# Decay from re-read rows of G, and k k^T with k q^T in one product, in an adaLN block with a gated delta rule

## The chip, the cores and the metric

The kernel runs on one core of one Trainium2 chip. The metric is the device time of one execution in microseconds (us), from start to end of the program; a profiled execution also has a span, from its first to its last instruction.

## What is computed

The block takes x of shape (8, 512, 256), 8 batch rows of 512 tokens, and computes two residual branches. The second is a small mixture of experts and is not touched. The first is gated attention with a delta rule, 16 key heads and 32 value heads of width 128:

```python
q = l2norm(q) * dk ** -0.5;  k = l2norm(k)         # each key head serves two value heads
G = cumsum(g) within a chunk
decay = where(tril, exp(G[..., :, None] - G[..., None, :]), 0.0)
A = -where(strict_tril, einsum(k_beta, k) * decay, 0.0)
T = solve_triangular(eye - A, eye, lower=True)
...
attn = where(tril, einsum(q_i, k_i) * decay, 0.0)
v_new = v_i - kcd_i @ state                        # v_i, kcd_i come from T
out_i = (q_i * exp(g_i)) @ state + attn @ v_new
```

q, k and v come from a projection of the normalised, modulated x, a causal convolution over four tokens, and SiLU; the output is normalised, gated with SiLU(z) and projected back. The kernel works with chunks of 128 tokens in place of the 64 of the reference (the result is the same), so each batch row has four chunks.

## The kernel before

Everything is fp32. The work is cut into 128 items: item n is key head `p = n % 16` of batch row `b = n // 16`, with its two value heads (h = 0, 1) and four chunks (c). One step n of the main loop (L1032 to L1069) runs five stages side by side, each for another item:

- `keys(n + 9)` (L481), the early stage: projection, convolution and SiLU of k (`projected`, L438), its transposes (`k_rows`), norms and scalars; the decays of the eight (chunk, head) pairs (`decay`, L521); k k^T (`products`, L539); their product on GpSimd (`decayed`, L551); and `leave` (L556), which writes the blocks to DRAM.
- one quarter of `diagonal_blocks` (L588) for a group of four items: the inverses of the 32x32 diagonal blocks, on VectorE, with one block in each partition. It reads the group back from DRAM in `begin` (L614); `join16_w` and `join16_x` (L664, L674) join 16-row pieces by a product and a reduction over 1024 or 2048 columns.
- `join(n + 1)` (L697): joining to 64 and 128 rows on TensorE.
- `queries(n + 1)` (L781), the late stage: projection of q and of two v, the squares and norms of q, k q^T (`products`, L819), its product with the causal mask `tri_le` (`qkm`) and with the decays (`s`, L835), and the transposes of v.
- `recur(n)` (L862), the recurrence over four chunks, and `finish(n - 1)` (L967): z, gating, the output projection (L1010).

`weave` (L38) merges the lists of steps by their relative position, so that the stages alternate in program order. Side steps (`beside`, L1025) carry the norms of the next batch row, before it is needed, and the experts of the last. The framework's planner then fixes one order for each engine's queue, from readiness of data, free buffers and program order; at run time each queue is in order. All loads and stores of the main loop go through SP's queue.

What the early stage makes for the late one goes through DRAM (pool `far`): `kfar` holds k and its transpose, `dfar` the decays, 512 KB an item. `load` of `queries` reads them back one step ahead of use.

The decay of two chunks is a TensorE product. GpSimd builds `gm` (L524), the mask times g, for 4 x 128 columns; a matmul with the mask `tri_gt` as stationary operand sums the g between two tokens (`ds`, L530); ScalarE takes Exp from PSUM (L532):

```python
nc.gpsimd.tensor_tensor(gm..., tri_le..., bc_last(rw["g"][:, 2 * gr : 2 * gr + 2, hs], P), ALU.mult)
mm(ps, tri_gt, gm.rearrange("p u i -> p (u i)"), start=True, stop=True)
nc.scalar.activation(dc.rearrange("p u i -> p (u i)"), ps, AF.Exp)
```

[...] The weights of k, of q and v (`key_weights`, `query_weights`, L423, L426) have two buffers each, z and output weights (`gate_weights`, L430) one. `out_weights` (L994) scales the output weights into a second tile `wg`.

Of the kernel before, what the change touches and what calls it, by code (L numbers as in the profile page):

```python
# [15 lines left out]
P = 128  # L16
# [32 lines left out]
def adaln_block(  # L49
# [62 lines left out]
    row = ctx.enter_context(tc.tile_pool(name="row", bufs=2))  # L112
    rows = {}
# [71 lines left out]
    def before_attention(b):  # L185
# [4 lines left out]
        def betas():  # L190
# [9 lines left out]
            d["g"] = row.tile([P, NC, HV], F32, name=f"g_{b}", tag="g")  # L200
# [27 lines left out]
        def decays():  # L228

            n = NC * HV  # L230
            ps = bank(ps_m, f"dec_{b}")
            gf = d["g"].rearrange("p c h -> p (c h)")
            for i, m in enumerate((tri_le, tri_gt, ones)):
                mm(ps[:, i * n : (i + 1) * n], m, gf, start=True, stop=True)
            ex = d["ex"] = row.tile([P, 3, NC, HV], F32, name=f"ex_{b}", tag="ex")
            nc.scalar.activation(ex.rearrange("p i c h -> p (i c h)"), ps[:, : 3 * n], AF.Exp)
            d["neg"] = row.tile([P, NC, HV], F32, name=f"neg_{b}", tag="neg")
            nc.vector.tensor_scalar_mul(d["neg"], ex[:, 0], -1.0)

        return [*norm_transposed(b, 0, 2, "a"), betas, soft, series, decays]  # L240
# [147 lines left out]
    with ExitStack() as st:  # L388
# [34 lines left out]
        def key_weights(n):  # L423
            weights(n, "wk", wp, ((HK + n % HK) * P, 1))

        def query_weights(n):  # L426
            p = n % HK
            weights(n, "wq", wp, (p * P, 1), ((2 * HK + 2 * p) * P, 2))
# [9 lines left out]
        def projected(n, parts):  # L438
# [5 lines left out]
            def one(wname, j, name, ch):  # L444
# [18 lines left out]
                def act():  # L463
                    pool = w2b if name == "q" else w1b
                    tag = "ka" if name == "k" else name
                    r = d[name] = pool.tile([P, SEQ], F32, name=f"{name}_{n}", tag=tag)
                    nc.scalar.activation(r, d["cv" + name], AF.Silu)  # L467
# [10 lines left out]
        def chunks_of(t):  # L478
            return bass.AP(t.tensor, t.offset, [[2 * NC * P, P], [1, 2 * NC * P]])

        def keys(n):  # L481
# [5 lines left out]
            def k_rows():  # L487
                ps = d["kt"] = bank(ps_m, f"kt_{n}")
                for c in range(NC):
                    nc.tensor.transpose(  # L490
                        ps[:, c * P : (c + 1) * P], d["k"][:, c * P : (c + 1) * P], ident
                    )
                kr = w1b.tile([P, NC, P], F32, name=f"kra_{n}", tag="kra")
                nc.scalar.copy(kr.rearrange("p c d -> p (c d)"), ps)
                d["kfar"] = far.tile([2, P, SEQ], F32, name=f"kfar_{n}", tag="kfar")
                nc.sync.dma_start(d["kfar"][0], d["k"])
                nc.sync.dma_start(d["kfar"][1], kr.rearrange("p c d -> p (c d)"))

            def norms():
                ps = d["kt"]  # L500
                nrm = d["nrmk"] = keep.tile([P, NC], F32, name=f"nrmk_{n}", tag="nrmk")
                for c in range(NC):
                    junk = w2b.tile([P, P], F32, name=f"jk_{n}_{c}", tag="jk")
                    nc.scalar.activation(
                        junk, ps[:, c * P : (c + 1) * P], AF.Square, accum_out=nrm[:, c : c + 1]
# [4 lines left out]
            def scalars():  # L510
# [10 lines left out]
            def decay(gr):  # L521

                gm = w1b.tile([P, 4, P], F32, name=f"gm_{n}_{gr}", tag="gm")
                nc.gpsimd.tensor_tensor(  # L524
                    gm.rearrange("p (c h) i -> p c h i", h=2),
                    tri_le.unsqueeze(1).unsqueeze(1).to_broadcast([P, 2, 2, P]),
                    bc_last(rw["g"][:, 2 * gr : 2 * gr + 2, hs], P), ALU.mult,
                )
                ps = bank(ps_m, f"ds_{n}_{gr}")
                mm(ps, tri_gt, gm.rearrange("p u i -> p (u i)"), start=True, stop=True)  # L530
                dc = d[f"dca{gr}"] = w2b.tile([P, 4, P], F32, name=f"dca_{n}_{gr}", tag="dca")
                nc.scalar.activation(dc.rearrange("p u i -> p (u i)"), ps, AF.Exp)  # L532
                if gr == 0:
                    d["dfar"] = far.tile([P, 2 * NC * P], F32, name=f"dfar_{n}", tag="dfar")
                nc.sync.dma_start(
                    d["dfar"][:, gr * SEQ : (gr + 1) * SEQ], dc.rearrange("p u i -> p (u i)")
                )

            def products():  # L539
                ps = bank(ps_m, f"kk_{n}")  # L540
                for c in range(NC):
                    cs = slice(c * P, (c + 1) * P)
                    mm(ps[:, cs], d["k"][:, cs], d["k"][:, cs], start=True, stop=True)
                v = ps.rearrange("p (c d) -> p c d", d=P)
                mt = d["mta"] = w1b.tile([P, 2 * NC, P], F32, name=f"mta_{n}", tag="mta")
                nc.vector.tensor_mul(  # L546
                    mt.rearrange("p (c h) i -> p c h i", h=2),
                    v.unsqueeze(2).to_broadcast([P, NC, 2, P]), bc_last(d["nb"], P),
                )

            def decayed(gr):  # L551
                us = slice(4 * gr, 4 * gr + 4)
                mt = d["mta"][:, us, :]
                nc.gpsimd.tensor_tensor(mt, mt, d[f"dca{gr}"], ALU.mult)  # L554

            def leave():  # L556
# [20 lines left out]
                nc.sync.dma_start(d["m6far"], mt[0:64, :, 64:128])  # L577

            return [
                *projected(n, [("wk", 0, "k", HK + p)]), k_rows, lambda: decay(0), norms, scalars,  # L580
                lambda: decay(1), products, lambda: decayed(0), lambda: decayed(1), leave,
# [6 lines left out]
        def diagonal_blocks(g):  # L588
# [25 lines left out]
            def begin():  # L614
# [4 lines left out]
                e["pr"] = w1b.tile([P, 2048], F32, name=f"prl_{g}", tag="prl")  # L619
# [32 lines left out]
            def join8_x(q):  # L652
                o = 16 * q
                wt = e["wt"][:, 64 * q : 64 * q + 64].rearrange("p (c b) -> p c b", c=8)
                pr = e["pr"][:, 1024 + 512 * q : 1536 + 512 * q].rearrange(
# [8 lines left out]
            def join16_w(k):  # L664

                pr = e["pr"][:, : 2048 >> k].rearrange("p (c a b) -> p c a b", c=8, a=16)
                mul(
                    pr, bc(minus_m(16, 8 * k, 16, 16 - 8 * k), 1, 8),
                    bc(part(yl, 8 * k, 8 * k, 8, 16 - 8 * k), 2, 16), ALU.mult,
                )  # L670
                wt = e["wt"].rearrange("p (c a) -> p c a", c=16)
                red(wt[:, 8 * k : 8 * k + 8, :], pr, AX.X, ALU.add)

            def join16_x(k):  # L674
                w = 8 + 8 * k
                pr = e["pr"][:, : 128 * w].rearrange("p (a c b) -> p a c b", a=8, c=16)
                wt = e["wt"].rearrange("p (c b) -> p c b", c=16)
                mul(
                    pr, bc(part(xl, 16 + 8 * k, 16, 8, w), 2, 16), bc(wt[:, :, :w], 1, 8), ALU.mult
                )  # L680
                red(part(xl, 16 + 8 * k, 0, 8, 16), pr, AX.X, ALU.add)

            def leave():
# [9 lines left out]
                [lambda: join16_w(0), lambda: join16_w(1)],  # L693
                [lambda: join16_x(0), lambda: join16_x(1), leave],
# [86 lines left out]
        def queries(n):  # L781

            b, p = divmod(n, HK)
            d, rw = its[n], rows[b]
            hs = slice(2 * p, 2 * p + 2)

            def load():
                d["k"] = w2b.tile([P, SEQ], F32, name=f"k_{n}", tag="k")
                nc.sync.dma_start(d["k"], d["kfar"][0])
                d["dc"] = w1b.tile([P, 2 * NC, P], F32, name=f"dc_{n}", tag="dc")  # L790
                nc.sync.dma_start(d["dc"].rearrange("p u i -> p (u i)"), d["dfar"])
                d["kr"] = w2b.tile([P, NC, P], F32, name=f"kr_{n}", tag="kr")
                nc.sync.dma_start(d["kr"].rearrange("p c d -> p (c d)"), d["kfar"][1])

            def squares():
                d["sq"] = w1b.tile([P, SEQ], F32, name=f"sq_{n}", tag="sq")
# [317 lines left out]
```

## Time and profile before

| | |
|---|---|
| median of 3 runs | 5013.29 us (5008.72 to 5019.26) |
| the profiled execution | 5009.07 us |
| its span | 5007.4 us |
| mean granted TensorE clock | 0.978 |
| GpSimd busy | 2128.2 us (43%) |
| DMA, SP's queue | 568.86 MB, 40.5% of 16 engines' span |

In a page of the profile PE is TensorE's matmuls, PEld its weight loads, DVE VectorE, ACT ScalarE, POOL GpSimd and SP the queue that issues DMAs. A row names line, engine, operation, result and sources, shapes and count; then the busy time in us and the mean ns of one; then the engine's idle time just before these instructions, and what ended it. Each fp32 matmul of the program shows as two records. `prq`, `prk` and `prv` are the banks of the projections of q, k and v, `op` that of the output.

### The profile page before, as it was taken

Reading aid. Unit: us, or ns where it says so; the run is one execution under the profiler, and the core shown is the slowest. Engines: PE = TensorE matmul, PEld = TensorE weight load, DVE = VectorE, ACT = ScalarE, POOL = GpSimd, SP = SyncE. Lnnn points to the kernel's source line nnn. Section 1 sums busy time; section 2 is a strip of 40 time slices with the busy share of each in tenths; the row PEclk is TensorE's granted clock in tenths of the full one; section 3 lists DMA queues with packets and bytes.
Section 4 is the critical chain, followed back from the end, with each engine's and each line's share of the span. In section 5 each row is a group of like instructions: output and inputs, shape, how many; then the busy total and the mean of one; then the engine's idle time right before and its main releaser. Section 6 shows DMA issues by size and latency. Waiting matters only on the chain. (4 is left out here: it accounts for less than half of the span.)

```text
span 5007.4 us, 86632 instructions
## 1 busy us (share of the span) xinstructions
PE 4749.6 (95%) x28800; PEld 3397.5 (68%) x28800; DVE 3799.0 (76%) x8080; ACT 3112.8 (62%) x8127; POOL 2128.2 (43%) x1962
## 2 busy tenths in 40 slices
PE   4799999999999999999999999999999999999998
PEld 2467776666776667766677666766766666776775
DVE  4777778877788777887777777877788776788754
ACT  3566666666666665666666676566666667656553
POOL 3344444444444434444444443444444444444432
PEclk8799999999999999999999999999999999999999
DMA  4344444444444444444344444444444444444331
GB/s 132 107 111 119 128 123 116 121 112 119 121 114 126 117 112 120 120 117 121 108 120 118 123 119 118 110 119 127 113 118 117 114 126 119 113 117 126 98 87 35
DMA packets 972522, 576.23 MB, mean 115 GB/s; under 512 B 656544, under 2 KB 836656, under 8 KB 972080
## 3 DMA queue, kind: packets, MB, share of 16 engines
q1 hardware_dynamic: 971264, 568.86, 40.5%
q8 instruction: 234, 3.83, 0.3%
q14 instruction: 208, 1.70, 0.1%
q10 hardware_dynamic: 816, 1.84, 0.1%
HBM read 356.53 MB, written 213.91 MB: 114 GB/s over the span
## 5 line engine op out<-in xcount | busy, mean ns | idle before, releaser
L952 ACT ACTIVATE jo<-o 128x128 f32<-128x128 f32 x1024 | 305.4, 299 | 679.9 <-DVE o L946 669.8
L458 DVE SCALAR_TENSOR_TENSOR cvv<-prv,cw,cvv 128x511 f32<-128x511 f32 (+2 forms) x768 | 556.7, 741 | 22.9 <-ACT cvv L456 20.3
L1010 PE MATMUL op<-wg,gt 128*128 128x256 f32 x2048 | 513.7, 390 | 10.9 <-DVE o L946 9.5
L524 POOL TENSOR_TENSOR gm<-tri_le,g 128x512 f32<-128x512 f32 x256 | 279.0, 1090 | 515.2 <-PE ds L530 505.1
L448 PE MATMUL prv<-ha,wq 128*128 128x512 f32 x1024 | 485.3, 596 | 3.0 <-DVE cvk L458 3.0
L977 PE MATMUL prz<-ha,wz 128*128 128x512 f32 x1024 | 485.6, 593 | 0.0
L797 POOL TENSOR_TENSOR sq<-q 128x512 f32<-128x512 f32 x128 | 133.0, 1039 | 793.9 <-ACT q L467 793.9
L554 POOL TENSOR_TENSOR mta<-mta,dca 128x512 f32<-128x512 f32 x256 | 325.3, 1287 | 341.6 <-DVE mta L546 199.9
L1010 PEld LDWEIGHTS op<-wg,gt 128*128 128x128 f32 x2048 | 373.2, 192 | 84.6 <-DVE o L946 14.6
L912 ACT ACTIVATE w<-u,br 128x128 f32<-128x128 f32 x1024 | 317.5, 363 | 147.4 <-PE u L897 121.1
L458 DVE SCALAR_TENSOR_TENSOR cvk<-prk,cw,cvk 128x511 f32<-128x511 f32 (+2 forms) x384 | 284.8, 742 | 159.5 <-ACT cvk L456 159.1
L835 POOL TENSOR_TENSOR s<-qkm,dc 128x256 f32<-128x256 f32 x512 | 373.5, 762 | 22.7 <-DVE qkm L826 18.2
L938 PEld LDWEIGHTS in<-w,s 128*128 128x128 f32 x2048 | 307.1, 192 | 109.0 <-issue 81.8
L467 ACT ACT_TABLE_LOAD x255 | 327.2, 1283 | 65.9 <-DVE cvk L458 42.0
L1015 DVE TENSOR_TENSOR xt<-xt,op 128x512 f32<-128x512 f32 x256 | 175.5, 685 | 250.3 <-PE op L1010 248.8
L532 ACT ACT_TABLE_LOAD x248 | 318.2, 1283 | 44.1 <-issue 36.2
L996 POOL TENSOR_TENSOR wg<-wo,ga 128x512 f32<-128x512 f32 x128 | 177.6, 1388 | 378.4 <-PE op L1010 377.3
L448 PEld LDWEIGHTS prv<-ha,wq 128*128 128x128 f32 x1024 | 192.5, 190 | 193.9 <-issue 180.9
L938 PE MATMUL in<-w,s 128*128 128x128 f32 x2048 | 319.1, 277 | 4.5 <-ACT xw L768 2.4
L530 PE MATMUL ds<-gm,tri_gt 128*128 128x512 f32 x512 | 281.0, 632 | 29.2 <-POOL gm L524 16.3
L992 POOL TENSOR_TENSOR o<-o,msq 128x512 f32<-128x512 f32 x256 | 304.4, 1210 | 10.0
L897 PEld LDWEIGHTS u<-r,y 128*128 128x128 f32 x1536 | 235.6, 194 | 94.4 <-issue 55.2
(214 smaller groups left out, 11861.9 us busy)
## 6 DMA issues: line engine op xcount, KB each, us to landing
dfar<-dca SPq DMA_DIRECT2D x256, 256.0 KB
dc<-dfar SPq DMA_DIRECT2D x128, 512.0 KB
wq<-in_dram SPq DMA_DIRECT2D x128, 256.0 KB
wz<-in_dram SPq DMA_DIRECT2D x128, 256.0 KB
wo<-in_dram SPq DMA_DIRECT2D x128, 256.0 KB
kfar<-k SPq DMA_DIRECT2D x128, 256.0 KB
kfar<-kra SPq DMA_DIRECT2D x128, 256.0 KB
k<-kfar SPq DMA_DIRECT2D x128, 256.0 KB
```

The costliest lines, as they stand in the source:

```text
L448: mm(ps, d[wname][:, kt, j * P : (j + 1) * P], hT[:, kt, :], start=kt == 0, stop=kt == NKT - 1,)
L458: nc.vector.scalar_tensor_tensor(a[:, s:], ps[:, : SEQ - s], cw[:, ch, 3 - s : 4 - s], a[:, s:], ALU.mult, ALU.add,)
L467: nc.scalar.activation(r, d["cv" + name], AF.Silu)
L532: nc.scalar.activation(dc.rearrange("p u i -> p (u i)"), ps, AF.Exp)
L554: nc.gpsimd.tensor_tensor(mt, mt, d[f"dca{gr}"], ALU.mult)
L835: nc.gpsimd.tensor_tensor(d["s"][:, u : u + 2, :], bc_mid(d["qkm"][:, c, :], 2), d["dc"][:, u : u + 2, :], ALU.mult,)
L912: nc.scalar.activation(w[:, h, :], ps[:, h * P : (h + 1) * P], AF.Copy, scale=d["br2"][:, c, h : h + 1],)
L938: mm(ps[:, h * P : (h + 1) * P], d["s"][:, 2 * c + h, :], cur["w"][:, h, :], start=True, stop=True,)
L952: nc.scalar.activation(junk, d["o"][:, c, h, :], AF.Square, accum_out=d["msq"][:, c, h : h + 1])
L977: mm(ps, d["wz"][:, kt, h * P : (h + 1) * P], hT[:, kt, :], start=kt == 0, stop=kt == NKT - 1,)
L992: nc.gpsimd.tensor_tensor(o, o, bc_last(m, P), ALU.mult)
L1010: mm(ps[:, k * DM : (k + 1) * DM], gt[h][:, c * P : (c + 1) * P], d["wg"][:, h, :], start=h == 0, stop=h == 1,)
```

## The change

The decays no longer come from a matmul. `decays` keeps G, the running sum of g within a chunk (`d["G"]`, tokens on partitions), transposes it on TensorE and writes the 128x128 result (a row for each chunk and head) to DRAM (`gfar`). For each item, `key_weights` reads the eight rows back, each copied to all 128 partitions (`gb`, one buffer). `decay` subtracts the token's own G by `tensor_scalar` on GpSimd, one instruction for each chunk and head, takes the minimum with 0, and ScalarE takes Exp in place, for both pairs of chunks in succession.

q moves from the late stage to the early one: projection, convolution, SiLU, squares, norms, scalars. k and q lie side by side in one tile `kqa` (one buffer), so one matmul with 256 columns gives k k^T and k q^T of a chunk. `products` and `decayed` work on two chunks at a time; `decayed` also makes s, which goes to DRAM (`sfar`) instead of the decays, as k and q do (`qfar`). The late stage, now `values`, has only v, and loads k with q, k's transpose, and s. To make room, `pr` of the diagonal blocks shrinks from 2048 to 1024 columns, `join16_w` and `join16_x` are cut in three pieces each, g has one buffer, and the output weights are scaled in place. `soft` and `series` become one side step.

```diff
@@ decays
+            d["G"] = row.tile([P, NC, HV], F32, name=f"G_{b}", tag="G")
+            nc.vector.tensor_copy(d["G"].rearrange("p c h -> p (c h)"), ps[:, :n])
+            ps = bank(ps_m, f"Gt_{b}")
+            nc.tensor.transpose(ps[:, :P], d["G"].rearrange("p c h -> p (c h)"), ident)
+            gt = row.tile([P, P], F32, name=f"Gt_{b}", tag="Gt", bufs=1)
+            nc.vector.tensor_copy(gt, ps[:, :P])
+            d["gfar"] = gfar.tile([P, P], F32, name=f"gfar_{b}", tag="gfar")
+            nc.sync.dma_start(d["gfar"], gt)
-        return [*norm_transposed(b, 0, 2, "a"), betas, soft, series, decays]
+        return [*norm_transposed(b, 0, 2, "a"), betas, lambda: (soft(), series()), decays]
@@ key_weights
-            weights(n, "wk", wp, ((HK + n % HK) * P, 1))
+            b, p = divmod(n, HK)
+            weights(n, "wk", wp, ((HK + p) * P, 1), (p * P, 1))
+            t = its[n]["gb"] = w1b.tile([P, NC, 2 * P], F32, name=f"gb_{n}", tag="gb")
+            far_g = rows[b]["gfar"]
+            nc.sync.dma_start(
+                t,
+                bass.AP(
+                    far_g.tensor, far_g.offset + 2 * p * P,
+                    [[0, P], [HV * P, NC], [1, 2 * P]],
+                ),
+            )
@@ keys
+            def squares():
+                d["sq"] = w1b.tile([P, NC, P], F32, name=f"sq_{n}", tag="sq")
+                nc.gpsimd.tensor_tensor(d["sq"], d["kqa"][:, :, 1, :], d["kqa"][:, :, 1, :], ALU.mult)
+                d["qfar"] = far.tile([P, 2 * SEQ], F32, name=f"qfar_{n}", tag="qfar")
+                nc.sync.dma_start(d["qfar"], d["kqa"].rearrange("p c k i -> p (c k i)"))
...
+            def decay():
+                for gr in range(2):
+                    dc = d[f"dca{gr}"] = w2b.tile([P, 2, 2, P], F32, name=f"dca_{n}_{gr}", tag="dca")
+                    for c in range(2):
+                        for h in range(2):
+                            k = 2 * p + h
+                            nc.gpsimd.tensor_scalar(
+                                dc[:, c, h, :], d["gb"][:, 2 * gr + c, h * P : (h + 1) * P],
+                                rw["G"][:, 2 * gr + c, k : k + 1], 0.0, ALU.subtract, ALU.min,
+                            )
+                for gr in range(2):
+                    f = d[f"dca{gr}"].rearrange("p c h i -> p (c h i)")
+                    nc.scalar.activation(f, f, AF.Exp)
+
+            def products(gr):
+                ps = bank(ps_m, f"kk_{n}_{gr}")
+                for c2 in range(2):
+                    c = 2 * gr + c2
+                    mm(
+                        ps[:, c2 * 2 * P : (c2 + 1) * 2 * P], d["kqa"][:, c, 0, :],
+                        d["kqa"][:, c].rearrange("p k i -> p (k i)"), start=True, stop=True,
+                    )
...
                 nc.vector.tensor_mul(
-                    v.unsqueeze(2).to_broadcast([P, NC, 2, P]), bc_last(d["nb"], P),
+                    d["mta"][:, us, :].rearrange("p (c h) i -> p c h i", h=2),
+                    v[:, :, 0, :].unsqueeze(2).to_broadcast([P, 2, 2, P]), bc_last(d["nb"][:, cs], P),
                 )
+                qkm = d[f"qkm{gr}"] = w2b.tile([P, 2, P], F32, name=f"qkm_{n}_{gr}", tag="qkm")
+                nc.vector.tensor_mul(qkm, v[:, :, 1, :], bc_mid(tri_le, 2))
 
             def decayed(gr):
-                nc.gpsimd.tensor_tensor(mt, mt, d[f"dca{gr}"], ALU.mult)
+                nc.gpsimd.tensor_tensor(mt, mt, dc.rearrange("p c h i -> p (c h) i"), ALU.mult)
+                for c in range(2):
+                    u = 4 * gr + 2 * c
+                    nc.gpsimd.tensor_tensor(
+                        d["sa"][:, u : u + 2, :], bc_mid(d[f"qkm{gr}"][:, c, :], 2), dc[:, c],
+                        ALU.mult,
+                    )
...
             return [
-                *projected(n, [("wk", 0, "k", HK + p)]), k_rows, lambda: decay(0), norms, scalars,
-                lambda: decay(1), products, lambda: decayed(0), lambda: decayed(1), leave,
+                *projected(n, [("wk", 0, "k", HK + p), ("wk", 1, "q", p)]), k_rows, decay, k_norms,
+                squares, k_scalars, lambda: products(0), q_norms, lambda: decayed(0),
+                lambda: products(1), q_scalars, lambda: decayed(1), leave,
             ]
@@ diagonal_blocks
-                [lambda: join16_w(0), lambda: join16_w(1)],
-                [lambda: join16_x(0), lambda: join16_x(1), leave],
+                [lambda: join16_w(0, 4, 0), lambda: join16_w(4, 4, 0), lambda: join16_w(8, 8, 8)],
+                [
+                    lambda: join16_x(0, 8, 8), lambda: join16_x(8, 4, 16),
+                    lambda: join16_x(12, 4, 16), leave,
+                ],
@@ values (was queries): load
+                kq = d["kq"] = w2b.tile([P, NC, 2, P], F32, name=f"kq_{n}", tag="kq")
+                nc.sync.dma_start(kq.rearrange("p c k i -> p (c k i)"), d["qfar"])
                 d["kr"] = w2b.tile([P, NC, P], F32, name=f"kr_{n}", tag="kr")
+                nc.sync.dma_start(d["kr"].rearrange("p c d -> p (c d)"), d["kfar"])
+                d["s"] = w2b.tile([P, 2 * NC, P], F32, name=f"s_{n}", tag="s")
+                nc.sync.dma_start(d["s"].rearrange("p u i -> p (u i)"), d["sfar"])
@@ out_weights
-                wg = d["wg"] = w1b.tile([P, 2, DM], F32, name=f"wg_{n}", tag="wg")
-                nc.gpsimd.tensor_tensor(wg, d["wo"], bc_mid(rw["ga"], 2), ALU.mult)
+                nc.gpsimd.tensor_tensor(d["wo"], d["wo"], bc_mid(rw["ga"], 2), ALU.mult)
```

## The prediction

> **What bounds the kernel now.** I read the page's busy line first, then a table of engine time by stretches, the groups by line, TensorE's timeline and last the list of waits. The page and the stretches (columns: length, then busy microseconds with instruction counts for PE, PEld, DVE, ACT, POOL, then TensorE clock, DMA share, GB/s):
>
> ```profile
> PE 4749.6 (95%) x28800; PEld 3397.5 (68%) x28800; DVE 3799.0 (76%) x8080; ACT 3112.8 (62%) x8127; POOL 2128.2 (43%) x1962
> ```
>
> ```profile
> 2040.08:2648.09 608.01, 589.95 (x3598) 423.52 (x3596) 473.07 (x1012) 391.15 (x1020) 264.86 (x244) 0.99 0.42 118
> 2110.15:2153.88 43.73, 41.74 (x240) 30.11 (x239) 34.30 (x81) 27.26 (x68) 15.76 (x16) 0.92 0.35 99
> 2191.55:2226.77 35.22, 34.82 (x210) 24.63 (x209) 28.33 (x62) 23.33 (x64) 16.11 (x15) 1.00 0.51 155
> 4800.00:4900.00 100.00, 100.00 (x640) 74.13 (x638) 57.11 (x125) 48.26 (x140) 29.63 (x31) 1.00 0.28 75
> ```
>
> The first stretch is 16 whole steps of the main loop in the steady state: 608.01 us, so 38.0 us a step, with PE busy 36.87, DVE 29.57, ACT 24.45, POOL 16.55 and DMA 0.42. The next two are single steps: one with much VectorE work (43.7 us) and one with little (35.2 us). The last has no early (`keys`) stage left: PE is busy throughout. Only PE is full, so an edit is worth what it takes off PE; the step with 34.3 us of DVE shows who is next.
>
> Now the rows of what the change touches (busy us, mean ns, then idle before and its releaser):
>
> ```profile
> L530 PE MATMUL ds<-gm,tri_gt 128*128 128x512 f32 x512 | 281.0, 632 | 29.2 <-POOL gm L524 16.3 <-DVE vr L848 9.9 <-ACT jk L504 2.1
> L524 POOL TENSOR_TENSOR gm<-tri_le,g 128x512 f32<-128x512 f32 x256 | 279.0, 1090 | 515.2 <-PE ds L530 505.1 <-DVE g L226 10.1
> ...
> L543 PE MATMUL kk<-k 128*128 128x128 f32 x1024 | 166.8, 306 | 1.7 <-DVE nrm L807 1.5 <-DVE vr L848 0.2
> ...
> L824 PE MATMUL qk<-q,k 128*128 128x128 f32 x1024 | 150.0, 281 | 3.2 <-DVE nrm L807 2.0 <-DVE g L202 1.3
> ...
> L532 ACT ACT_TABLE_LOAD x248 | 318.2, 1283 | 44.1 <-issue 36.2 <-PE ds L530 2.8 <-DMA xw<-lx 0.3
> ```
>
> Each matmul of the program is two records. But a busy PE waits too. The timeline shows how fast it can go:
>
> ```profile
> 2522.44 1.16 PE L543 MATMUL kk<-k 128*128 128x128 f32 x8
> 2523.43 1.06 PE L824 MATMUL qk<-q,k 128*128 128x128 f32 x8
> ...
> 2526.51 1.89 PE L1010 MATMUL op<-wg,gt 128*128 128x256 f32 x8
> 2528.24 0.61 PE L897 MATMUL u<-r,y 128*128 128x128 f32 x4
> ...
> 2532.57 1.88 PE L448 MATMUL prq<-ha,wq 128*128 128x512 f32 x4
> 2534.29 1.88 PE L448 MATMUL prk<-ha,wk 128*128 128x512 f32 x4
> ```
>
> From start to start, 4 records of 512 columns take 1.72 us (0.430 each), 8 of 256 columns 1.73 (0.216 each), 8 of 128 columns 0.99 for k k^T and 0.90 for k q^T. The same 512-column record is charged 281.0/512 = 0.549 us in the ds row. The difference is waiting that is booked as busy. Last, the list of waits (who waited for whom: us in total, times, longest):
>
> ```profile
> POOL sq L797 <- ACT q L467: 793.9, 128, 10.5
> ...
> POOL gm L524 <- PE ds L530: 505.1, 219, 8.1
> POOL wg L996 <- PE op L1010: 377.3, 121, 12.7
> ```
>
> GpSimd waits, for TensorE among others; no large wait in that list has TensorE waiting for GpSimd.
>
> **What the Trainium skill says.** Perfetto Trace Analysis, Identifying the Most-Contended Engine, says that matmul busy share is a poor measure of how near TensorE is to its limit. The trace agrees (0.549 against 0.430), so I use both as ends. GPSIMD Engine Reference, 4.1 Engine selection, says that a one-input elementwise operation on GpSimd runs roughly at line rate and a two-input one about half as fast. The trace agrees: a 128x256 copy took 0.40 us, a 128x256 two-input product 0.762. DMA: Bandwidth & Descriptors, Why small descriptors are slow, puts a fixed cost on each packet; the packet records show 46 ns (median) for 1 KB, 84 for 2 KB, 159 for 4 KB.
>
> **The change, part by part, for one steady step.**
>
> Decay products. Two matmuls of 512 columns leave PE: 4 records, 4 x 0.430 = 1.72 us at least, and (281.0 + 29.2)/128 = 2.42 us if the row and the idle before it go whole.
>
> One 256-column product. kk and qk take 0.99 + 0.90 = 1.89 us by spacing, (166.8 + 150.0)/128 = 2.48 by rows. Four matmuls of 256 columns are 8 records, 1.73 us by the op row's spacing. Gain 0.16 to 0.75 us. The sum off PE is 1.88 to 3.17 us; I take the middle, 2.5, since the ds pair stood behind POOL (its list of waits has both PE behind gm and gm behind PE).
>
> VectorE. mta goes from one 128x1024 (1222 ns) to two 128x512; the nearest row from PSUM is vr with 681, so +0.14. qkm from 683 to two of 128x256 at 418 (wd): +0.15. The 16-row joins split 2048 columns into twice 1024: products 3 x 1.989 instead of 3.725 + 1.989, the other three pairs likewise +0.15, +0.15 and +0.14, together +0.69 in four steps, +0.17 a step. DVE rises by 0.46 to 30.0 us. It costs nothing where DVE has slack and up to 0.46 in the steps that DVE fills; the smaller pieces let others in between, which may give some back. I take 0.2.
>
> GpSimd. Two gm (1.09 each) leave, eight `tensor_scalar` 128x128 come. No such row exists; nearest is the mask set-up, 128x128 with one input, 0.29 us, and above it the two-input 128x256 with 0.762. Eight cost 2.3 to 6.1 us; I take 2.4. POOL then has 16.8 (at most 20.5) of 35.7 us, off the path; its other pieces (mta, s, sq, norms) move with their stage and keep their sizes. What they feed is read again one step later at the earliest (`begin` of `diagonal_blocks`, for the last of four) and otherwise up to eight steps later; that hides them. Where the cover is gone, as in the first steps, they cost their 2.4 us.
>
> ScalarE. The two Exp now stand together, so of four table changes a step (503 loads in all) two go: 2 x 1.283 = 2.6 us less, 24.45 to 21.9. ACT is not the bound: 0 on the path.
>
> DMAs and SP's queue. Out: two decay writes (256 packets of 2 KB), k out and in (256 of 2 KB), decay in (128 of 4 KB): 512 x 84 + 128 x 159 = 63 us, 4.0 us on each of 16 engines. In: the G rows to 128 partitions (512 packets of 1 KB), kq out and in and s out and in (512 of 4 KB): 512 x 46 + 512 x 159 = 105 us, 6.6. So +2.6 us, from 16.0 to 18.6 of 35.7: half full, hidden by the eight steps of lead. SP issues five fewer and five more. The new wait: the G rows have one buffer, so the load for the next step waits on SP until POOL has made this step's decays, and behind it queue weights for v, z and output, join loads and write-outs. The load's own time is 1.5 us over 16 engines and, were all 512 reads of the same 4 KB taken one by one, 512 x 46 = 23.6 us, still under a step. SP has some 31 issues of about 0.4 us, 13 of 38 us, so there is room; 0, up to 4 us if it starves PE. The output weights are scaled in place, so their load now waits for the last projection (L1010) instead of POOL's wg: a load of 128 packets behind a wait that POOL had before (377.3 us in the list of waits); 0.
>
> Sum: 2.5 - 0.2 = 2.3 us a steady step. There are 119 of these (n = 0 to 118): -274 us.
>
> Ends. The first nine steps run the early stage alone; k's transposes follow each other there at 59.80, 73.58, 90.47, ... 157.94 us, 16.4 us apart, with PE idle. q joins: one more projection, three more shifts on DVE (0.74 each) and one more SiLU (0.64), partly beside k's own chain, while the wait for gm goes (2.11 us in these steps). I take +2 us a step, 0 to +5: +18. G's transpose and trip to DRAM: +3; for later rows it is hidden, since `soft` and `series` are now one side step and `decays` so comes one step earlier. The last nine steps lose q: projection 1.72, norm sums 0.81, product 0.90 = 3.4 us each, PE being full there: -31.
>
> Total -274 + 18 + 3 - 31 = -284. The profiled execution took 5009.07 us (span 5007.4); it becomes 4725, and with the median 4.2 above it, 4729. I say 4730.
>
> **The rivals.**
> (B) The rows go whole. For: DVE's long pieces are halved, the tables leave ACT. Against: waits booked as busy tend to reappear at the next matmul. 3.17 x 119 = 377, ends as above: 5013 - 377 - 10 = 4626.
> (C) DVE takes over. For: in 8 of the 16 steps it is busy over 31 us, in one 36.44 of 37.67; these can't shrink. Against: on average it has 8 us free. Half of the gain, the 0.46 in the other half: -137 + 27 - 10 = -120, 4893.
> (D) Slower: SP's queue is held by the one G buffer. It needs POOL to come late to the decays (it idles in program order behind sq, 793.9 us in the list of waits) and a weight or join load behind it to be due within that time. It decides once PE loses more than 2.3 us a step; at 4 us, (4 - 2.3) x 119 - 10 = +192, 5205. Against: SP's waits hardly show as PE waits now.
> (E) No change: gain and loss meet, 5013.
>
> **Chances.** A 0.47, B 0.20, C 0.18, D 0.11, E 0.04. Faster than 0.2% (about what a measurement of this kernel can tell from none) are A, B, C: 0.85; slower D: 0.11. A alone spans 4670 to 4790 (PE 1.9 to 2.8 a step, ends +-25). The range reaches to B and most of C: 4610 to 4890.
>
> **What would show it.** A step near 35.7 us; no ds and gm rows; kk with 1024 records of 256 columns at about 0.22 to 0.25 us; tensor_scalar at 0.3 us on POOL; table loads halved; DVE near 30 us a step; DMA share near 0.5. It is wrong if SP's or DMA's names stand before PE rows (D), if PE drops under 90% with DVE as releaser (C), or if a tensor_scalar takes over 1 us.

## The result and the profile after

The changed kernel took 5518.12 us (median of 4 runs, 5507.98 to 5521.62) against 5013.32 before: a ratio of 1.1003 (95% interval 1.0984 to 1.1022). It was forecast at 4730, in a range of 4610 to 4890, and is 10% slower.

The page of the changed kernel, then 16 whole steps of its steady state (the columns are those of the table shown before):

```profile
PE 4793.4 (87%) x27272; PEld 3371.5 (61%) x27272; DVE 3814.9 (69%) x8480; ACT 2839.7 (51%) x7895; POOL 2586.5 (47%) x2730
...
POOL dca L569 12%; PE prv L468 6%; POOL sa L606 6%; PE prk L468 4%; POOL mta L603 4%; PE in L947 3%; PE op L1018 3%; PE prz L986 3%; PE u L906 3%; PE prq L468 3%; PE dst L929 2%; PE py L811 2%; PE w L789 2%; POOL nrm L541 2%; PE pi L884 1%
```

```profile
2294.52:2963.56 669.04, 588.57 (x3406) 414.79 (x3405) 475.86 (x1062) 353.53 (x986) 326.02 (x339) 0.95 0.49 132
```

TensorE has fewer matmul records (27,272 against 28,800) and is no longer full: 87% busy against 95%. A step takes 669.04/16 = 41.8 us against 38.0. GpSimd has 25% of the chain that ended last, and its row `dca`, the eight `tensor_scalar`, leads it. (The chain of the kernel before broke off after 8% of the span, so it can't be compared.) The rows and the longest waits:

```profile
L569 POOL TENSOR_SCALAR dca<-gb,G 128x128 f32<-128x128 f32 x1024 | 754.1, 753 | 45.1 <-DMA gb<-gfar 23.1
...
L947 PE MATMUL in<-w,s 128*128 128x128 f32 x2048 | 353.3, 297 | 240.9 <-ACT w L921 240.2
...
L582 PE MATMUL kk<-kqa 128*128 128x256 f32 x1024 | 295.5, 405 | 16.9 <-ACT kqa L492 15.9 <-DVE nrm L540 0.8 <-DVE cvv L478 0.3
```

```profile
ACT dca L575 <- POOL dca L569: 1117.2, 250, 7.4
...
PE in L947 <- ACT w L921: 240.2, 76, 6.0
```

Exp waits 1117 us in total for GpSimd, and TensorE's `in` (the last product of a chunk in the recurrence) waits for ScalarE's `w` (weighing u in the recurrence). Before, Exp waited next to nothing, and `in` too:

```profile
L532 ACT ACTIVATE dca<-ds 128x512 f32<-128x512 f32 x256 | 152.9, 597 | 18.4 <-PE ds L530 15.6
...
L938 PE MATMUL in<-w,s 128*128 128x128 f32 x2048 | 319.1, 277 | 4.5 <-ACT xw L768 2.4 <-DVE gt L1003 2.1
```

Added up over the list of waits, TensorE waits 401 us for ScalarE and 308 for VectorE, against 76 and 149 before, and 2 us for GpSimd itself. One end of a step shows how the waits belong together. The timelines of GpSimd, ScalarE and TensorE, each from the changed kernel (start, length, engine, line, operation, count; in brackets the idle time before and what ended it):

```profile
2539.17 1.27 POOL L603 TENSOR_TENSOR mta<-mta,dca 128x512 f32<-128x512 f32 x1
2540.40 1.41 POOL L606 TENSOR_TENSOR sa<-qkm,dca 128x256 f32<-128x256 f32 x2
2541.90 2.78 POOL L569 TENSOR_SCALAR dca<-gb,G 128x128 f32<-128x128 f32 x4
```

```profile
2544.72 0.63 ACT L575 ACTIVATE dca<-dca 128x512 f32<-128x512 f32 x1 [4.85 <-POOL dca L569]
2545.25 0.61 ACT L897 ACTIVATE tmp<-pi,egq 128x128 f32<-128x128 f32 x2
2545.75 0.37 ACT L921 ACTIVATE w<-u,br 128x128 f32<-128x128 f32 x1
```

```profile
2537.80 0.71 PE L906 MATMUL u<-r,y 128*128 128x128 f32 x4
...
2539.54 1.89 PE L1018 MATMUL op<-wo,gt 128*128 128x256 f32 x8
2546.17 1.52 PE L947 MATMUL in<-w,s 128*128 128x128 f32 x4 [4.73 <-ACT w L921]
```

GpSimd makes four decays of the next item, 2.78/4 = 0.695 us each. Ahead of them stand `mta` and `sa` of the item before: they read the `dca` tile that the new decays go into (it has two buffers, one for each pair of chunks). ScalarE has reached the Exp of these decays in its queue and stands still for 4.85 us. Behind Exp wait `tmp` and `w` of the recurrence, whose own data were there (`u` was done at 2538.5). `w` comes, and only then TensorE goes on, 4.73 us late. GpSimd's `mta` reads the result of this Exp at 2579.8, 35 us later. So it seems that the loss is not GpSimd's work as such: an Exp that nobody needs for long stands ahead of work that TensorE needs at once. The experiments test this.

### The profile page after: what moved, and what is told of

Read it like the earlier page. It is cut to its first block, busy times and chain, and to the rows that moved or that the text cites. A ratio compares the mean times of both kernels' runs of the same rounds, so it can differ in the third digit from the quotient of the medians.

```text
span 5518.6 us, 83876 instructions
## 1 busy us (share of the span) xinstructions
PE 4793.4 (87%) x27272; PEld 3371.5 (61%) x27272; DVE 3814.9 (69%) x8480; ACT 2839.7 (51%) x7895; POOL 2586.5 (47%) x2730
## 4 chain that ended last, share of the span: by engine, by line
PE 37%; POOL 25%; issue 16%; DVE 7%; ACT 5%; DMA 4%; SPq 2%; POOLq 0%; DVEq 0%; ACTq 0%
POOL dca L569 12%; PE prv L468 6%; POOL sa L606 6%; PE prk L468 4%; POOL mta L603 4%; PE in L947 3%; PE op L1018 3%; PE prz L986 3%; PE u L906 3%; PE prq L468 3%; PE dst L929 2%; PE py L811 2%; PE w L789 2%; POOL nrm L541 2%; PE pi L884 1%
## 5 line engine op out<-in xcount | busy, mean ns | idle before, releaser
L1018 PE MATMUL op<-wo,gt 128*128 128x256 f32 x2048 | 581.7, 426 | 224.8 <-DVE gt L1011 124.3
L569 POOL TENSOR_SCALAR dca<-gb,G 128x128 f32<-128x128 f32 x1024 | 754.1, 753 | 45.1 <-DMA gb<-gfar 23.1
L1018 PEld LDWEIGHTS op<-wo,gt 128*128 128x128 f32 x2048 | 407.9, 211 | 331.1 <-DVE gt L1011 148.2
L996 POOL TENSOR_TENSOR msq<-msq,mhalf 128x8 f32<-128x8 f32 x128 | 241.3, 1885 | 766.0 <-DVE msq L995 734.2
L947 PE MATMUL in<-w,s 128*128 128x128 f32 x2048 | 353.3, 297 | 240.9 <-ACT w L921 240.2
L468 PE MATMUL prv<-ha,wv 128*128 128x512 f32 x1024 | 500.8, 612 | 2.3 <-DVE cvk L478 2.1
L606 POOL TENSOR_TENSOR sa<-qkm,dca 128x256 f32<-128x256 f32 x512 | 373.5, 749 | 3.4 <-DVE qkm L597 3.4
L478 DVE SCALAR_TENSOR_TENSOR cvq<-prq,cw,cvq 128x511 f32<-128x511 f32 (+2 forms) x384 | 284.9, 742 | 61.7 <-ACT cvq L476 59.6
L468 PEld LDWEIGHTS prv<-ha,wv 128*128 128x128 f32 x1024 | 197.7, 202 | 206.8 <-issue 201.9
L468 PE MATMUL prk<-ha,wk 128*128 128x512 f32 x512 | 321.4, 750 | 1.5 <-ACT sv_gb L127 1.5
L906 PE MATMUL u<-r,y 128*128 128x128 f32 x1536 | 304.9, 302 | 7.0 <-DVE r L892 6.0
```

The lines of the kernel that those rows point to most:

```text
L468: mm(ps, d[wname][:, kt, j * P : (j + 1) * P], hT[:, kt, :], start=kt == 0, stop=kt == NKT - 1,)
L478: nc.vector.scalar_tensor_tensor(a[:, s:], ps[:, : SEQ - s], cw[:, ch, 3 - s : 4 - s], a[:, s:], ALU.mult, ALU.add,)
L569: nc.gpsimd.tensor_scalar(dc[:, c, h, :], d["gb"][:, 2 * gr + c, h * P : (h + 1) * P], rw["G"][:, 2 * gr + c, k : k + 1], 0.0, ALU.subtrac ...
L606: nc.gpsimd.tensor_tensor(d["sa"][:, u : u + 2, :], bc_mid(d[f"qkm{gr}"][:, c, :], 2), dc[:, c], ALU.mult,)
L906: mm(ps[:, h * P : (h + 1) * P], d["y"][:, 2 * c + h, :], r[:, h, :], start=True, stop=True,)
L947: mm(ps[:, h * P : (h + 1) * P], d["s"][:, 2 * c + h, :], cur["w"][:, h, :], start=True, stop=True,)
```

## The experiments

The main theory (ACT-queue): the two Exp wait in ScalarE's queue for slow GpSimd instructions, with the recurrence behind them. Rival 1 (GpSimd-busy): GpSimd's own later work comes late. Rival 2 (early-stage): q's move, the trips through DRAM and the single buffers cost the time.

"Step" is the mean distance of the norm powers `msq` of items 16 to 112, 37.96 us before. The base is the kernel before on the same chip (5011 to 5017 us in all calls). Runs given without a ratio were timed once; repeats of one variant here lie up to 0.6% apart.

| run | what differs | us | step us | Exp's wait for its GpSimd decays |
|---|---|---|---|---|
| before | | 5013 | 37.96 | |
| after | | 5518 | 41.93 | 1117 |
| e1_no_sub | no subtraction | 4868 | 36.72 | |
| e2_late_exp | Exp made to depend on later data | 5013 | 37.79 | none listed |
| e3_dve, e9_dve_3 | decays on VectorE | 4926, 4917 | 37.30, 37.27 | |
| e4_old_ds | TensorE decay, q early | 5109 | 38.72 | |
| e5_before_room | before, with the room edits | 5038 | 38.34 | |
| e6_before_newdecay | before, with the new decay | 5447 | 41.36 | 875 |
| e7_double | every decay twice | 5991 | 45.45 | 1627 |
| e8_tt | two wider GpSimd instructions | 5206 | 39.19 | 822 |
| e10_dve_wg | e3, output weights apart | 4911 | 37.28 | |
| e11_act_sub, e16_act_sub_3 | subtraction on ScalarE | 4897, 4889 | 36.71, 36.65 | |
| e12_before_dve | before, decays on VectorE | 4966 | 37.70 | |
| e13_exp_pos | Exp later in the program only | 5278 | 39.90 | 1097 |
| e14_act_sub_wg | e11, output weights apart | 4924 | 37.07 | |

**Is it the decays at all?** e1 leaves the subtraction and the minimum out.

```diff
-  nc.gpsimd.tensor_scalar(dc[:, c, h, :], d["gb"]..., rw["G"]..., 0.0, ALU.subtract, ALU.min)   # x8
-  nc.scalar.activation(f, f, AF.Exp)
+  nc.scalar.activation(f, d["gb"][:, 2 * gr : 2 * gr + 2, :].rearrange("p c j -> p (c j)"), AF.Exp)
```

> The changed kernel without the subtraction and the minimum on GpSimd: Exp reads the rows of G directly, so the decays are not those of the reference; all else stays. Theory ACT-queue (the two Exp stand in ScalarE's queue ahead of the recurrence's work and wait for eight slow tensor_scalar on GpSimd): GpSimd loses 6 us a step and Exp waits for a load only, so 4700 to 4850 us, and the wait of Exp for GpSimd (1117 us) is gone. Rival GpSimd-busy (what stands behind the decays in GpSimd's own queue comes late): the same, 4700 to 4850. Rival early-stage (q in the early stage, the trips through DRAM and the single buffers cost the time, not the decays): 5350 or more.

Measured 4867.89 us, just over the expected range: the decays on GpSimd cost 650 us of 5518. Rival 2 falls as the main cause. The busy line of this run, its 16 steps and one of its waits:

```profile
PE 4579.7 (94%) x27272; PEld 3246.6 (67%) x27272; DVE 3759.6 (77%) x8480; ACT 2830.1 (58%) x7891; POOL 1825.4 (38%) x1706
```

```profile
2010.53:2594.13 583.60, 561.36 (x3407) 398.92 (x3406) 468.24 (x1061) 352.58 (x987) 227.31 (x212) 1.00 0.57 152
```

```profile
ACT dca L568 <- POOL sa L601: 563.5, 213, 5.6
```

TensorE has 35.1 us of busy time a step and the step lasts 36.5 us. Exp still waits, 563 us in all, for `sa` to free its buffer (more buffers were not tried). Yet the whole is fast, and TensorE waits 94 us for ScalarE in all, not 401: a wait in front of Exp does harm only by what is behind it at that moment.

The loss can be divided. The two profiled executions differ by 652 us. TensorE's idle time (span less busy) is 725 us in the changed kernel and 287 here: 439 us. The rest is busy time, 4793.4 against 4579.7 us for the same 27,272 records: 214 us, which go with the clock (see below).

**GpSimd's work or ScalarE's queue?** e2 keeps all GpSimd work. It gives Exp a scale operand of 1.0 that VectorE writes after `k_scalars`, so that Exp can't be queued earlier.

```diff
+  one = d["one"] = sm.tile([P, NC, 2], F32, name=f"one_{n}", tag="one")
+  nc.vector.tensor_scalar(one, nb, 0.0, 1.0, ALU.mult, ALU.add)            # in k_scalars
-  nc.scalar.activation(f, f, AF.Exp)                                       # in decay
+  nc.scalar.activation(f, f, AF.Exp, scale=d["one"][:, 0, 0:1])            # a step of its own, after k_scalars
```

> The changed kernel with the same eight tensor_scalar on GpSimd, but both Exp a step of their own behind k_scalars, made to depend on it by a scale operand of 1.0 that VectorE writes there (one tiny VectorE instruction a step more). Theory ACT-queue: by the time ScalarE reaches Exp the decays are long done, the wait of 1117 us falls under 300, and the time to 4750 to 4950 us. Rival GpSimd-busy: GpSimd does as much as before, 5400 to 5550. Rival early-stage: 5400 to 5550.

Measured 5013.07 us: 505 us of the 650 go, though not down to the 4950 that the theory allowed. Its rows:

```profile
L571 POOL TENSOR_SCALAR dca<-gb,G 128x128 f32<-128x128 f32 x1024 | 832.4, 829 | 43.7 <-DMA gb<-gfar 22.9
...
L579 ACT ACTIVATE dca<-dca,one 128x512 f32<-128x512 f32 x256 | 173.3, 716 | 1.8
...
L607 POOL TENSOR_TENSOR mta<-mta,dca 128x512 f32<-128x512 f32 x256 | 335.0, 1309 | 628.6 <-ACT dca L579 313.4 <-DVE mta L596 68.3 <-DMA wz<-in_dram 66.1
```

GpSimd is no less busy with decays than in the changed kernel (832 us), and Exp's idle time is 1.8 us instead of 1117; the table load just before Exp waits 82.7 us for `one`. TensorE's waits for ScalarE fall from 401 to 69 us. The GpSimd-busy rival falls for the main part. `mta` on GpSimd now waits for Exp instead (313.4 us), so the edit may have a price of its own: the 145 us that are left to e1 are not divided between this price and GpSimd's work.

**A quicker producer.** e3 puts the same eight instructions on VectorE (`nc.vector` for `nc.gpsimd`); e9 repeats it in rounds.

> The changed kernel with the eight tensor_scalar on VectorE instead of GpSimd. At some 0.2 to 0.4 us each they are 2 to 3 us on VectorE a step. Theory ACT-queue: Exp still stands where it stood but its producers are quick; 4750 to 4950 us. Rival GpSimd-busy: the same, 4750 to 4950. Rival early-stage: 5400 or more.

> The kernel with the decays on VectorE once more, timed in rounds: 4920 to 4935 us.

Measured 4926.27, as expected, then 4916.96 us (ratio 0.9809, 0.9791 to 0.9827), 3 us under its range: faster than the kernel before. Two rows of e9:

```profile
L569 DVE TENSOR_SCALAR dca<-gb,G 128x128 f32<-128x128 f32 x1024 | 300.2, 342 | 15.8 <-POOL sa L606 12.0 <-DMA gb<-gfar 3.9
...
L575 ACT ACTIVATE dca<-dca 128x512 f32<-128x512 f32 x256 | 156.8, 626 | 3.3 <-DVE dca L569 1.5
```

An instruction takes 300.2/1024 = 0.293 us of VectorE, and Exp no longer waits (3.3 us; the table load before it waits 75.6 us for the decays).

**The parts apart.** e4 keeps q early and takes the old TensorE decay back. e5 is the kernel before with only the edits that make room. e6 is the kernel before with only the new decay, and the output weights in place for room.

```diff
 # e4, in decay
-  nc.gpsimd.tensor_scalar(...)                                             # x8
+  nc.gpsimd.tensor_tensor(gm..., tri_le..., bc_last(rw["g"][:, 2 * gr : 2 * gr + 2, hs], P), ALU.mult)
+  mm(ps, tri_gt, gm.rearrange("p u i -> p (u i)"), start=True, stop=True)
+  nc.scalar.activation(dc.rearrange("p c h i -> p (c h i)"), ps, AF.Exp)
 # e5, against the kernel before
-  e["pr"] = w1b.tile([P, 2048], F32, name=f"prl_{g}", tag="prl")
+  e["pr"] = w1b.tile([P, 1024], F32, name=f"prl_{g}", tag="prl")           # joins in three pieces
-  nc.gpsimd.tensor_tensor(wg, d["wo"], bc_mid(rw["ga"], 2), ALU.mult)
+  nc.gpsimd.tensor_tensor(d["wo"], d["wo"], bc_mid(rw["ga"], 2), ALU.mult)
 # e6, against the kernel before, in decay(gr)
-  mm(ps, tri_gt, gm.rearrange("p u i -> p (u i)"), start=True, stop=True)
+  nc.gpsimd.tensor_scalar(dc[:, 2 * c + h, :], d["gb"]..., rw["G"]..., 0.0, ALU.subtract, ALU.min)   # x4
```

> The changed kernel with the old decay: mask times g on GpSimd, TensorE product, Exp from PSUM (g has two buffers again, the G rows are not loaded). So the q move, the 256-column product and the trips through DRAM alone. Theories ACT-queue and GpSimd-busy: the loss goes with the decays, and what is left is the merged product and fewer table loads against more DMA: 4930 to 5050 us. Rival early-stage: 5350 or more, since all it blames is still there and TensorE has the decay product on top.

> The kernel before with only the edits that make room: output weights scaled in place, pr of 1024 columns, the 16-row joins in three pieces. If these are what the early-stage structure loses (about 100 us, by the run with the old decay), 5080 to 5120 us; if it is q's move and its trips, 5000 to 5035.

> The kernel before with only the decay changed: rows of G re-read, eight tensor_scalar on GpSimd, Exp behind each four as the old decay had it (output weights in place, for room); q stays in the late stage. Theory ACT-queue: the loss needs no q in the early stage; Exp again waits for GpSimd several us at a time with the recurrence behind it, against 2 us a step that leave TensorE: 5050 to 5450 us, with over 500 us of waiting of Exp for GpSimd. Rival (the decays hurt only where GpSimd has q's squares and products around them): 4850 to 4950.

e4 measured 5109.06 us, above the 5050 of the main theory: the early stage does cost something next to the old decay. e5 measured 5037.6 (ratio 1.0047, 1.003 to 1.0064), just above the 5035 of "it is q's move". The room edits cost some 20 us, and q's move, with its trips through DRAM and the merged product, 71 more. e6 measured 5447.48, at the upper edge: the loss needs no q in the early stage.

```profile
ACT dca L553 <- POOL dca L548: 875.4, 245, 12.9
...
PE in L959 <- ACT w L933: 236.3, 68, 6.8
```

The same pair of waits stands in this kernel, 875 us of Exp for GpSimd and 236 us of `in` for `w`, against 1117 and 240 in the changed one.

**Dose.** e7 issues each `tensor_scalar` twice, which changes no value. e8 replaces the four of a group by two wider ones.

```diff
 # e8
+  nc.gpsimd.tensor_tensor(dc, d["gb"]..., bc_last(rw["G"][:, cs, hs], P), ALU.subtract)
+  nc.gpsimd.tensor_scalar_min(f, f, 0.0)
```

> The changed kernel with every tensor_scalar of the decays issued twice (the same result). Theory ACT-queue: each group of four now holds Exp 2.8 us longer, some 5 to 6 us a step, most of it on the path, 6000 to 6300 us, with Exp's waits for GpSimd over 1700 us. Rival, that the eight instructions cost little by themselves: under 5650.

> The changed kernel with the decays on GpSimd in two forms: one two-input subtraction of 512 columns with G broadcast along them, and one minimum with an immediate of 512 columns, in place of four tensor_scalar of 128 columns with a pointer. If the price of the pointer form lies in each instruction (0.7 us for 128 columns), the subtraction takes 1.0 to 1.3 us as other products of that size do and the minimum 0.5 to 0.8; 3.4 us a step instead of 5.6. Theory ACT-queue: Exp waits less, 5150 to 5350 us. If the price is per column, no gain: 5450 to 5600.

e7 measured 5991.48 (just under its range), e8 5206.19 us. Exp's waits in e8 and e7:

```profile
ACT dca L575 <- POOL dca L572: 821.9, 247, 7.4
```

```profile
ACT dca L579 <- POOL dca L573: 1627.3, 256, 13.2
```

From e8 over the changed kernel to e7, Exp's wait rises by 295 and 510 us, and the time by 312 and 473: at this end nearly one for one. e7's wait, 1627, is a little under the 1700 expected. e8's price per instruction was not as expected:

```profile
L572 POOL TENSOR_SCALAR dca<-dca 128x512 f32<-128x512 f32 x256 | 392.7, 1535 | 19.8
...
L567 POOL TENSOR_TENSOR dca<-gb,G 128x512 f32<-128x512 f32 x256 | 281.7, 1101 | 40.4 <-DMA gb<-gfar 22.8
```

The subtraction takes 1.10 us, but the one-input minimum of 512 columns 1.53. Both together are (392.7 + 281.7)/128 = 5.3 us a step against 754.1/128 = 5.9, so GpSimd gained little and the time fell by 312 us all the same. The wider form also changes the planned order, and which of the two did it isn't settled.

**Who sets the place of Exp in its queue?** e13 puts the Exp where e2 has it in the program, without the operand.

```diff
-  (in decay) nc.scalar.activation(f, f, AF.Exp)
+  (a step of its own, after k_scalars) nc.scalar.activation(f, f, AF.Exp)
```

> The changed kernel with the two Exp at the later place in program order that the run with late Exp gave them, but without the scale operand: nothing but the eight tensor_scalar has to be ready. If the place in program order sets ScalarE's queue, 4990 to 5040 us as in that run. If the planner moves an Exp up to where it believes its data ready, whatever its place, 5400 to 5550 us, and Exp waits for GpSimd over 900 us again.

Measured 5277.98 us, between the two. Exp waits 1097 us as in the changed kernel, so it is still queued too early and the place in the program does not hold it back; but TensorE's `in` waits only 37.2 us for `w` instead of 240.2:

```profile
ACT dca L577 <- POOL dca L569: 1096.7, 251, 8.8
...
PE u L908 <- ACT y L837: 116.2, 51, 3.7
...
PE in L949 <- ACT w L923: 37.2, 19, 3.8
```

Of ScalarE's work it is now `y`, a copy that `u` needs, that TensorE waits for most (116.2 us). In all it waits 260 us for ScalarE, between the 401 of the changed kernel and the 69 of e2. The same wait of Exp costs 240 us less with other work behind it. So the 505 us of e2 are two parts: 240 from the new place in the program, with Exp's wait as long as ever, and 5277.98 - 5013.07 = 265 from the operand, which ends that wait. That the planner takes GpSimd's instructions for quicker than they are is the reading that fits this order; its own figures were not looked at, so this is argued and not shown.

**A version that beats both.** e10 is e3 with the output weights in a tile of their own. e11 and e16 put the subtraction on ScalarE and the minimum on VectorE; e14 joins the two edits. e12 is e6 with VectorE in place of GpSimd.

```diff
 # e11, e16, e14 (d["G"] holds -G)
-  nc.gpsimd.tensor_scalar(...)                                             # x8
+  nc.scalar.activation(dc[:, c, h, :], d["gb"]..., AF.Identity, bias=rw["G"][:, 2 * gr + c, k : k + 1])   # x8
+  nc.vector.tensor_scalar_min(f, f, 0.0)                                   # x2
 # e10, e14
-  nc.gpsimd.tensor_tensor(d["wo"], d["wo"], bc_mid(rw["ga"], 2), ALU.mult)
+  wg = d["wg"] = w1b.tile([P, 2, DM], F32, name=f"wg_{n}", tag="wg")
+  nc.gpsimd.tensor_tensor(wg, d["wo"], bc_mid(rw["ga"], 2), ALU.mult)
```

> The kernel with the decays on VectorE and the scaled output weights in a tile of their own again (for room the transposed G uses the buffers of the normalised x). The edits that made room cost the kernel before 20 us; if that was the output weights (GpSimd's wait for their load, 473 us in the run on VectorE), 4895 to 4915 us; if it was the three-piece joins, 4920 to 4935 as without this edit.

> The changed kernel with the subtraction on ScalarE (Identity with -G as bias, eight of 128 columns, some 0.36 us each) and the minimum on VectorE (two of 512 columns); GpSimd has none of it. Theory ACT-queue: no slow producer stands before Exp, ScalarE has room for 2.9 us a step: 4870 to 4960 us. Rival, that any work in front of Exp delays the recurrence as much as it takes: 5050 or more.

> The version with the subtraction on ScalarE, timed in rounds: 4890 to 4905 us, below the decays on VectorE (4917) and below its twin with the output weights apart (4924).

> The best variant so far (subtraction on ScalarE, minimum on VectorE; 4897 us in one run) with the output weights in a tile of their own: 4880 to 4900 us, a few us less than without, as on VectorE (6 us).

> The kernel before with only the decay changed and made on VectorE (output weights in place; q stays in the late stage). The decay product's 2.0 to 2.4 us a step leave TensorE, VectorE gains 2.4 us. If q's move costs some 70 us, as the run with the old decay says against the one with the room edits alone, this beats the same decays in the changed structure: 4840 to 4900 us. If q's move pays once the decays are cheap: 4950 to 5000.

e10 measured 4910.56 us (ratio 0.9798, 0.978 to 0.9815): 6 us under e9, within what the two intervals leave open. e11 measured 4896.91 and e16 4889.13 us (ratio 0.9769, 0.9746 to 0.9792), the best of all, 11.4% less than the changed kernel (5518.12). e14 came out at 4923.72 (0.9815, 0.9799 to 0.9831), above the 4880 to 4900 expected: slower than e16, where the edit went with 6 us less in e10. It seems that single edits of this kind shift the planned order by tens of us, so a difference of that size is no evidence on what its edit is worth. e12 measured 4965.54 (0.9903, 0.988 to 0.9925), above e9 by 49 us: in the second of its two ranges, and against the 71 us of e4 and e5. By these runs q's move costs 71 us beside the old decay and pays 49 beside the new one. But e12 also lacks the three-piece joins of e9 and has each Exp behind its own four decays, and both figures have the size of a mere shift of order. Why the sign turns is open.

## Why the prediction was wrong, step by step

**The step that failed** is GpSimd's. The prediction put the eight instructions at 2.4 us with an upper bound of 6.1 and wrote "off the path": what they feed "is read again one step later at the earliest ... that hides them". The size was near the upper bound (754.1/128 = 5.9 us), but that alone was inside the sum's cover. What failed is the cover. The first reader is not one step later: it is Exp, on a queue that the recurrence shares. The prediction priced ScalarE by its table loads, wrote "0 on the path", and asked only who uses the results, not who stands behind the instruction that waits. The sum had 0 for this. The decays on GpSimd cost 650 us by e1, and 505 of these hang on where Exp stands and what it depends on, by e13 and e2.

None of the signs that the prediction named points there. No `tensor_scalar` takes over 1 us on average (0.753). TensorE did fall under 90%, but ScalarE is the releaser named most, not VectorE as in rival C.

**The rival that ended slower** had the right shape and the wrong queue. It put the stall in SP's queue, behind the one buffer of the G rows. The changed kernel's trace shows that to be small:

```profile
SPq L439 <- POOL dca L569: 16.4, 6, 5.7
```

16.4 us in all, and 23.1 us of GpSimd waiting for the load of G. TensorE waits 4.4 us for DMAs in the whole kernel. One sum of the prediction is off, without effect here: 1.9 us a step with the ends 25 us higher gives 5013 - (1.9 - 0.2) x 119 - 10 + 25 = 4826 for the slow end of outcome A, not 4790.

**What leaves TensorE.** The prediction took 2.5 us a step, between 1.88 (spacing) and 3.17 (rows). The 16 steps of e1 shown above have 36.87 - 35.09 = 1.8 us less busy time. But of the six such stretches from item 16 to item 112 they are the least busy of e1, and those shown before are the busiest of that kernel. All six together, in the kernel before and in e1:

```profile
825.91:4470.17 3644.26, 3530.84 (x21577) 2530.34 (x21576) 2833.79 (x6046) 2347.37 (x6110) 1587.25 (x1456) 0.99 0.42 118
```

```profile
835.13:4360.66 3525.53, 3385.06 (x20430) 2405.22 (x20429) 2814.40 (x6347) 2115.45 (x5916) 1362.33 (x1264) 0.99 0.57 150
```

That is (3530.84 - 3385.06)/96 = 1.5 us less busy time a step, under the lower bound. The merged product brought 316.8 - 300.2 = 17 us over the kernel (0.13 a step), a little under its lower bound of 0.16. With the 281.0 us of the decay product, 298 us of rows left, but TensorE's busy time fell by 4749.6 - 4579.7 = 170: waiting booked as busy did come back at other matmuls, as the argument against the full-gain rival said. Idle time grew from 1.18 to 1.46 us a step, so the step fell by 1.24 us only. So even with free decays this structure gives 4868, not 4730: this term was too large as well.

**VectorE.** +0.46 us was forecast, +0.17 measured ((475.86 - 473.07)/16). Most new rows came out near their prices (`mta` 683 ns, `qkm` 414, the largest join product 1967 against 1989); one join product is above (1285 against 1213). Where the gap lies was not traced.

**ScalarE's tables** fell to about half, as forecast: 140 and 120 loads where 255 and 248 stood.

**The ends.** The last steps went from 32.3 to 28.6 us, -3.7 against -3.4 forecast. The first `msq` power comes at 252 us in e1 against 233 before, +19 against +21 forecast; in the changed kernel itself at 294, 42 us after e1, which leaves the decays out.

**TensorE's clock** was not in the sum. For the same work (3406 and 3407 records in 16 steps), TensorE is busy 588.57 us in the changed kernel and 561.36 in e1, with granted clocks of 0.95 and 1.00: 27.2/16 = 1.7 us of the 5.3 us by which these steps differ. Over the whole kernels, busy time times mean granted clock is 4793.4 x 0.934 = 4477 in the changed kernel and 4579.7 x 0.978 = 4479 in e1, so the lower clock accounts for the 214 us of longer busy time. The Trainium skill, TensorE: Matmul & The Clock Gate, What's actually happening, says that an idle stretch throttles the array's clock. The traces agree in direction: 287 us of idle time go with 0.978 (e1), 371 with 0.965 (e2), 592 with 0.952 (e13), 725 with 0.934 (the changed kernel). By this reading the waits are paid twice, as idle time and as slower matmuls.

## What to carry to other kernels

When work is moved to an idle engine, look past its results to the instruction that waits for them: list what stands behind that one in its own in-order queue, and price the wait by that. Where a planner fixes the order, a wrong price for one instruction may come back as a wrong order on another engine (here argued, not shown). A true dependency held Exp back where its place in the program did not. A wait in the list is no loss by itself: 563 us of it were harmless in one kernel, and equal waits of 1100 us differed by 240 us in another pair.

## What the runs showed of the hardware that was not expected

A GpSimd `tensor_scalar` with one tensor input was no cheaper than a two-input product. For 128 columns it took 754.1/1024 = 0.736 us on average and 0.70 at its shortest, as much as the two-input `sa` of 256 columns (373.5/512 = 0.73). For 512 columns with an immediate it took 1.53, while a two-input subtraction of 512 columns took 1.10. VectorE's own work doesn't explain it: in the changed kernel those that follow each other start 0.689 us apart (median) whether VectorE is idle or busy meanwhile. The statement in the Trainium skill, GPSIMD Engine Reference, 4.1 Engine selection, that one-input work runs roughly at line rate, on which the prediction's 0.3 us leaned, compares GpSimd with VectorE. For these two forms it does not hold: VectorE took 0.293 us for the first, and 118.8/256 = 0.46 (in e16) for the minimum of 512 columns. The measurement decides.
